# A graph layer with a fast Fourier convolution: PSUM tiles written whole before they are read, filter groups in tiles of their own, and one more adjacency turned by matrix multiply

## The chip, the cores and the metric
The kernel runs on one NeuronCore of a Trainium2 chip. The metric is the device time of one execution in microseconds; before the change the median of 14 runs is 1843.53 us (1836.01 to 1849.42). TensorE is PE in the profile, VectorE DVE, ScalarE ACT, GpSimd POOL, SyncE SP. SP computes nothing here: it only issues transfers. POOL issues transfers too, and ACT a few at the start.

## The reference
All data are float32. There are 64 graphs of 256 nodes with 256 features. Each is normalised and cut at zero, h = max(layernorm(x), 0), and then passes one layer:

```
xc  = transpose(h)                                  # features x nodes
c   = relu(bn1(conv1d(xc, conv1_w, 1 tap)))
c   = bn2(conv1d(c, conv2_w, 17 taps, pad 8))
x_conv = transpose(relu(c + xc))
s   = h @ w_se.T + b_se                             # 3 numbers per node
A   = exp(-|s_n - s_m|^2) * adj
x_nmp = A @ relu(h @ w_msg.T + b_msg)
gi  = concat(x_conv, x_nmp) @ w_ih.T + b_ih ; gh = h @ w_hh.T + b_hh
r, z = sigmoid(gi_r + gh_r), sigmoid(gi_z + gh_z)
n   = tanh(gi_n + r * gh_n)
out = x + (1 - z) * n + z * h
```

## The kernel before, in words
Graphs go in pairs (32 pairs) and batches of four pairs (8 batches). A batch's 17-tap convolution is done in a transformed domain: `split` and `forward` (VectorE) turn the output of the first convolution, `product` (TensorE) multiplies each of the 47 pieces of the spectrum with its filter matrix, and `branch_back`, `odd_back`, `q_back`, `p_back` and `join` (VectorE) turn back. `begin(m)` and `complete(m)` hold the products. Every product needs its own 256 KB matrix out of device memory, fetched by `load_kinds` (line 848) into one of nine slots named wb; a slot is loaded again when the product that used it is done.

**The filter matrices** are made at the start: `filters` (line 826) does two matmuls of the taps with constant points into a PSUM tile, ScalarE copies the tile to one of six buffers named fo, and a transfer, by turns from SP and POOL, writes it to device memory (filt). There are 57 such steps, taken from one list by `filter_steps` (line 1161) between other work.

**PSUM** is cut into four one-bank tiles (aux) and two two-bank tiles (acc), each kind handed out in a ring (lines 546 and 547). The dependencies are kept by tile: whoever writes one bank of an acc tile waits for the reader of its other bank.

**The adjacency.** `affinity(i)` (line 961) forms exp(-distance) on ScalarE and multiplies it by the adjacency on VectorE. The aggregation needs the product turned. For pairs below BY_DMA (line 589) the adjacency comes in as it is (`load_adj`, two transfers of 256 KB into the tile adj), and the product is turned on TensorE: eight 128x128 transposes and two ScalarE copies into the tile adjh (lines 975 to 982), where `aggregate` (line 986) reads it. For the other pairs the adjacency itself is turned on its way in: `turn_adj` (line 592) issues from SP a transposing transfer into the tile halves and four transfers to device memory (halves_d), `load_adj` fetches these into adjh with four transfers from POOL, and `join_adj` (line 610) makes the tile adj of them with two ScalarE copies.

**What sets the order of the work.** Every operation is first recorded, with its dependencies, and issued later by `emit`. The first `emit(True)` (line 1196), which covers the setup with the first four pairs' `transpose_h`, `conv1` and `split` and the first filter steps, issues in the order of the record. The other two calls (1209: the rest of the setup; 1361: all eight batches at once) go by a planner (line 375): it keeps a clock for each engine and issues whichever ready operation can start first, on each engine the one with the earliest due time. An operation on which nothing waits and which waits for nothing is ready from the beginning of its call, wherever it was recorded. `turn_h` (line 758) uses the tile halves too, so all transposing transfers follow one another in the order of the record.

Of the kernel before, what the change touches and what calls it, by code (L numbers as in the profile page):

```python
# [461 lines left out]
def kernel(  # L462
# [26 lines left out]
    DC = D // P  # L489
# [26 lines left out]
    def keep(name, *dims):  # L516
        return const.tile([P, *dims], FP, name=name)
# [28 lines left out]
    aux = Ring(psum.tile([P, W], FP, name=f"aux{k}") for k in range(4))  # L546
    acc = Ring(psum.tile([P, 2, W], FP, name=f"acc{k}") for k in range(2))
# [38 lines left out]

    BY_DMA = 3
    ADJD = {}  # L590

    def turn_adj(i):
        if i >= NP:
            return
        nc.sync.dma_start_transpose(out=halves, in_=adj[G * i:G * (i + 1)].rearrange("g n m -> (g n) m").bitcast(U16))
        ADJD[i] = halves_d()
        v = ADJD[i].rearrange("h q (k a) n -> k a (h q) n", a=4)
        for k in range(2 * MC):
            nc.sync.dma_start(out=v[k], in_=halves[:, k])

    def load_adj(i, eng=nc.gpsimd):
        if i >= NP:
            return
        if i < BY_DMA:
            load_rows(adj_rows, adj, i, eng)
            return
        for q in range(2 * MC):
            eng.dma_start(out=adjh[:, q], in_=ADJD[i][:, q])

    def join_adj(i):  # L610
        if not BY_DMA <= i < NP:
            return
# [174 lines left out]
    def conv1(i, both=None):  # L787
        if i >= NP:
            return
        p = acc() if both else None  # L790
        for o in range(DC):
            q = p[:, o] if both else aux()
            for k in range(DC):
                mm(q, w_c1[:, k, o * P:(o + 1) * P], HT[i][:, k, :], start=(k == 0), stop=(k == DC - 1))
            v = h1.rearrange("p (g o) s b -> p o g s b", o=DC)[:, o, :, :, 1:1 + NW]
            u = q.rearrange("p (g s b) -> p g s b", g=G, b=NW)
            if i == 0:
                nc.vector.tensor_scalar(v, u, s1[:, o:o + 1], h1_shift[:, o:o + 1], ALU.mult, ALU.add)
                nc.vector.tensor_scalar(v, v, 0.0, None, ALU.max)
            else:  # L800
                nc.scalar.activation(v, u, AF.Relu, bias=h1_shift[:, o:o + 1], scale=s1[:, o:o + 1])
# [159 lines left out]
    def affinity(i):  # L961
# [9 lines left out]
        for g in range(G):  # L971
            for c in range(MC):
                e = e_tile[:, g, c].rearrange("p (c h b) -> p c h b", c=MC, b=NW)
                nc.vector.tensor_mul(e, e, adj_rows[:, g * MC + c].rearrange("p (b h c) -> p c h b", c=MC, b=NW))
        if i < BY_DMA:
            at = adjh.bitcast(FP).rearrange("p a n -> p (a n)").rearrange("p (g c n) -> p g c n", g=G, c=MC)
            for g in range(G):
# [4 lines left out]
                nc.scalar.copy(at[:, g].rearrange("p c n -> p (c n)"), q)  # L982
        if i + 1 < BY_DMA:
            load_adj(i + 1)

    def aggregate(i):
# [3 lines left out]
        at = e_tile  # L990
        if i < BY_DMA:
            at = adjh.bitcast(FP).rearrange("p a n -> p (a n)").rearrange("p (g c n) -> p g c n", g=G, c=MC)
# [163 lines left out]
    FIRST = PARTS[1][1]  # L1156
    steps = deque((m, g) for g in range(FIRST) for m in range(len(PASSES)))
    steps.extend((m, g) for m in range(len(PASSES)) for g in range(FIRST, NG))
    banks = [0, None]

    def filter_steps(n):
        for _ in range(n):
            k = banks[0] % 4
            if k == 1:
                banks[1] = acc()
            banks[0] += 1
            p = aux() if k % 2 == 0 else banks[1][:, k // 2]
            filters(p, *steps.popleft(), nc.gpsimd if len(steps) % 2 else nc.sync)

    norm(0)  # L1170
# [5 lines left out]
    for j in range(PB):  # L1176
        if j > 0:
            transpose_h(j)
        if 0 < j < PB - 1:
            norm(j + 1)  # L1180
        if j == 2:
            nc.gpsimd.dma_start(out=w_msg[:, :, D:], in_=se_wT.rearrange("(k p) s -> p k s", p=P))
            for t, v in ((b_msg[:, :D], msg_b), (b_msg[:, D:], se_b)):
                nc.gpsimd.dma_start(out=t, in_=bass.AP(tensor=v.tensor, offset=v.offset, ap=[[0, P], [1, v.shape[0]]]))
            nc.sync.dma_start(out=w_msg[:, :, :D], in_=msg_wT.rearrange("(k p) o -> p k o", p=P))
            load_adj(0, nc.sync)
        conv1(j, True)
        if j == 2:
            *bn2, b_ih, b_hh = columns("bn2")
            s2, h2_shift = fold_bn(bn2, "bn2", 1.0 / L)  # L1190
            b_rz = keep("b_rz", 2 * DC)
            nc.vector.tensor_add(b_rz, b_ih[:, :2 * DC], b_hh[:, :2 * DC])
            nc.vector.tensor_scalar(b_rz, b_rz, 0.5, None, ALU.mult)
        split(j)
        filter_steps((4, 4, 2, 2)[j])
    nc.emit(True)
    load_x(PB)
    forward(0)
# [20 lines left out]
    for b in range(NB):  # L1219
        i = b * PB  # L1220
        nxt = i + PB
        if b > 0:
            finish(i - 1)
        begin(0)
        begin(1)
        complete(0)
        if b > 0:
            embed(i)
        complete(1)
        fft.branch_back(Yv, T, 0)  # L1230
        begin(2)
        if b > 0:
            affinity(i)
            load_adj(i + 1)
            give("tz0", "tz1")
        begin(3)
        complete(2)
        complete(3)
        if b == 0:
            norm(nxt)  # L1240
        fft.branch_back(Yv, T, 2)
        fft.odd_back(Yv, T)
        aggregate(i)
        begin(4)
        begin(5)
        if b > 0:
            join_adj(i + 1)
        else:
            nc.gpsimd.dma_start(out=w_hh, in_=hh_wT.rearrange("(k p) o -> p k o", p=P))
            nc.gpsimd.dma_start(out=w_ih, in_=ih_wT.rearrange("(k p) o -> p k o", p=P))  # L1250
            weight_sums()
        complete(4)
        message(i + 1)
        complete(5)
        fft.q_back(Yu, T)
        fft.odd_factors(Yv)
        begin(6)
        begin(7)
        embed(i + 1)
        if b == 0:  # L1260
            transpose_h(nxt)
            load_x(nxt + 1)
        else:
            join_h(nxt)
        complete(6)
        affinity(i + 1)
        if b > 0:
            load_adj(i + 2)
        complete(7)
        fft.p_back(Yu, T)  # L1270
        fft.q_factors(Yu)
        roles()
        sums(i, "h")
        sums(i, "xn")
        join(i)
        join(i + 1)
        if b == 0:
            turn_adj(3)
        stats(nxt + 1)
        aggregate(i + 1)  # L1280
        if b > 0:
            join_adj(i + 2)
        message(i + 2)
        conv1(nxt)
        split(nxt)
        turn_h(nxt + 1)
        embed(i + 2)
        sums(i, "xc")
        if b == 0:
            load_y(0)  # L1290
        else:
            load_adj(i + 3)
        sort_h(nxt + 1)
        turn_adj(nxt)
        join(i + 2)
        join(i + 3)

        def between():
            affinity(i + 2)
            join_h(nxt + 1)  # L1300
            stats(nxt + 2)
        gates(i, between)
        finish(i)
        for n in IN:
            sums(i + 1, n)
        conv1(nxt + 1)
        split(nxt + 1)
        if b + 1 < NB:
            forward(0)
        turn_h(nxt + 2)  # L1310
        aggregate(i + 2)
        if b == 0:
            load_adj(i + 3)
        sort_h(nxt + 2)
        turn_adj(nxt + 1)

        def between():
            join_h(nxt + 2)
            join_adj(i + 3)
            message(i + 3)  # L1320
            stats(nxt + 3)
        gates(i + 1, between)
        finish(i + 1)
        for n in IN:
            sums(i + 2, n)
        conv1(nxt + 2)
        split(nxt + 2)
        turn_h(nxt + 3)
        sort_h(nxt + 3)
        turn_adj(nxt + 2)  # L1330
        embed(i + 3)

        def between():
            affinity(i + 3)
            join_h(nxt + 3)
            conv1(nxt + 3)
            split(nxt + 3)
            if b + 1 < NB:
                forward(1)
            stats(nxt + 4)  # L1340
        gates(i + 2, between)
        finish(i + 2)
        turn_h(nxt + 4)
        aggregate(i + 3)
        for n in IN:
            sums(i + 3, n)
        sort_h(nxt + 4)
        turn_adj(nxt + 3)
        load_adj(nxt)
        if b + 1 < NB:  # L1350
            pending.extend(TURNS)

        def between():
            join_adj(nxt)
            message(nxt)
        gates(i + 3, between)
        give("axn", "axc", "ah")
        give("bh", "bxn", "bxc", "e")
        load_kinds()
# [47 lines left out]
```

## Time and profile before

| | |
|---|---|
| median of 14 runs | 1843.53 us (1836.01 to 1849.42) |
| profiled execution: device time, span of its trace | 1842.78 us, 1840.9 us |
| busy PE, DVE, ACT, POOL | 1733.7, 1505.1, 910.1, 240.6 us |
| PE busy in 0 to 120 us, 120 to 190 us, 190 to 300 us | 87.72, 60.21, 101.37 us |
| PE busy in seven windows of 210 us from 300 to 1770 us | 200.93 to 206.50 us |
| mean granted TensorE clock | 0.981 of full speed |

The span is the time from the first to the last instruction of the trace; 1.9 us of the device time lie around it. Nearly all operations are recorded through one helper, so all of them carry its line, L361, and are told apart by the tiles that they write and read: "acc<-V,wb" is a product of begin or complete, "acc<-hT,w_c" the first convolution, "aux<-taps,points" a filter step, "halves<-in_adj" the transposing transfer of turn_adj. A row of a timeline gives the start, the time taken, the operation with its count, and in brackets how long the engine stood idle before it and whom it waited for. "SPq" rows are SP's issuing of transfers, not the transfers themselves. A matmul in float32 shows as two records, so one product of 4 matmuls is 8 records.

### The profile page before, as it was taken

To read this page: it belongs to the slowest core of one execution; us is meant where nothing else is said; L and a number is where in the kernel's file an instruction comes from. 1 tells how busy PE (TensorE), PEld (TensorE's weight loads), DVE (VectorE), ACT (ScalarE), POOL (GpSimd) and SP (SyncE) were. 2 spreads that over 40 slices of the span, in tenths; PEclk is the share of its full clock that TensorE was granted. 3 is DMA by queue.
4 is the path that set the end of the run, shared out by engine and by line. 5 is a ranking of instruction groups with operands and counts; after the bars stand their busy time and mean duration, and the time that the engine had idled before them with its cause. 6 is when DMAs were issued, how large, how long until landed. Compare 5 with 4: busy or idle time off the path is not lost.

```text
span 1840.9 us, 26618 instructions
## 1 busy us (share of the span) xinstructions
PE 1733.7 (94%) x9190; PEld 1455.0 (79%) x9190; DVE 1505.1 (82%) x3462; ACT 910.1 (49%) x1763; POOL 240.6 (13%) x357
## 2 busy tenths in 40 slices
PE   4979989999999999999999999999999999999996
PEld 2659777787888878898878878888878878888885
DVE  3777987869978899789979799789979699789643
ACT  1544634455445564357454554447544564446331
POOL 2220031111011011011111100110211100110000
PEclk9999999999999999999999999999999999999998
DMA  7698245693347724494445824474444933264001
GB/s 182 196 213 252 63 110 116 162 246 79 81 108 191 212 48 107 87 279 110 110 110 169 237 64 88 107 228 145 108 112 119 266 100 81 58 189 138 24 23 35
DMA packets 250505, 246.25 MB, mean 134 GB/s; under 512 B 142936, under 2 KB 176500, under 8 KB 250371
## 3 DMA queue, kind: packets, MB, share of 16 engines
q1 hardware_dynamic: 216634, 183.83, 38.2%
q0 software_dynamic: 30784, 58.07, 12.6%
q10 hardware_dynamic: 2953, 2.66, 0.7%
q8 instruction: 72, 1.18, 0.3%
q14 instruction: 62, 0.51, 0.1%
HBM read 156.56 MB, written 44.30 MB: 109 GB/s over the span
## 4 chain that ended last, share of the span: by engine, by line
PE 50%; DVE 35%; DMA 7%; ACT 4%; issue 4%; SPq 1%; POOL 0%; ACTq 0%; DVEq 0%; POOLq 0%
PE acc L361 35%; PE aux L361 15%; DVE V L361 9%; DVE T L361 6%; DVE wb L361 3%; DVE U L361 3%; DVE tr L361 3%; DMA x<-in_x_dram 3%; DVE gn L361 3%; DMA wb<-filt 2%; DVE acc L361 2%; DVE msg L361 1%; DVE y L361 1%; DVE PT L361 1%; DVE Yv L361 1%
## 5 line engine op out<-in xcount | busy, mean ns | idle before, releaser
L361 PE MATMUL acc<-wb,w_ih 128*128 128x256 f32 x768 | 197.9, 380 | 0.0
L361 PEld LDWEIGHTS acc<-wb,w_ih 128*128 128x128 f32 x768 | 146.2, 190 | 20.0
L361 PE MATMUL aux<-wb,w_x 128*128 128x256 f32 x576 | 144.0, 382 | 4.7 <-DVE msg L361 3.6
L361 PE MATMUL acc<-wb,w_x 128*128 128x256 f32 x576 | 138.6, 383 | 5.9 <-DVE acc L361 5.9
L361 PE MATMUL acc<-V,wb 128*128 128x128 f32 x1024 | 130.9, 286 | 9.9 <-DMA wb<-filt 9.9
L361 DVE SCALAR_TENSOR_TENSOR V<-T,V 128x128 f32<-128x128 f32 (+2 forms) x448 | 138.7, 376 | 0.0
L361 PEld LDWEIGHTS acc<-V,wb 128*128 128x128 f32 x1024 | 128.0, 203 | 12.8 <-DMA wb<-filt 10.5
L361 PEld LDWEIGHTS acc<-wb,w_x 128*128 128x128 f32 x576 | 107.2, 190 | 35.7 <-DVE acc L361 15.6
L361 POOL DMA_DIRECT2D out_dram<-y x62 | 38.0, 616 | 732.3 <-DVE y L361 704.7
L361 PE MATMUL aux<-w_msg,hT 128*128 128x259 f32 x512 | 129.7, 383 | 0.6 <-ACT e L361 0.4
L361 PEld LDWEIGHTS aux<-wb,w_x 128*128 128x128 f32 x576 | 107.6, 190 | 28.3 <-DVE msg L361 6.7
L361 PE MATMUL acc<-hT,w_hh 128*128 128x256 f32 x384 | 110.1, 387 | 13.3 <-ACT acc L361 7.5
L361 PEld LDWEIGHTS acc<-U,wb 128*128 128x128 f32 x1024 | 119.2, 192 | 2.6 <-issue 1.3
L361 PE MATMUL acc<-U,wb 128*128 128x128 f32 x1024 | 120.8, 275 | 0.0
L361 POOL DMA_DIRECT2D adjh<-halves_d x116 | 69.1, 603 | 375.8 <-ACT adj L361 365.5
L361 PE MATMUL aux<-e,msg 128*128 128x256 f32 x464 | 114.5, 387 | 1.0 <-DVE e L361 1.0
L361 PE MATMUL acc<-wb,w_hh 128*128 128x256 f32 x384 | 110.4, 381 | 3.4 <-DVE acc L361 3.4
L361 PE MATMUL acc<-Yv,w_ih 128*128 128x256 f32 x384 | 110.1, 382 | 1.6 <-ACT Yv L361 1.6
L361 PE MATMUL aux<-hT,w_c 128*128 128x512 f32 x224 | 109.1, 595 | 2.1 <-ACT e L361 1.4
L361 DVE TENSOR_TENSOR acc<-acc,wb 128x512 f32<-128x512 f32 x64 | 44.3, 692 | 80.0 <-PE acc L361 79.8
L361 PE MATMUL acc<-xnm,w_ih 128*128 128x256 f32 x384 | 106.8, 380 | 0.0
L361 DVE BATCH_NORM_STATS2 st<-x 128x6 f32<-128x256 f32 x116 | 44.2, 417 | 76.6 <-DMA x<-in_x_dram 76.6
(175 smaller groups left out, 3877.6 us busy)
## 6 DMA issues: line engine op xcount, KB each, us to landing
wb<-filt SPq DMA_DIRECT2D x376, 256.0 KB
y<-in_x_dram POOLq DMA_DIRECT2D x64, 256.0 KB, 4.5
out_dram<-y POOLq DMA_DIRECT2D x62, 256.0 KB, 5.8
x<-in_x_dram SPq DMA_DIRECT2D x58, 256.0 KB
halves_d<-halves SPq DMA_DIRECT2D x116, 128.0 KB
adjh<-halves_d POOLq DMA_DIRECT2D x116, 128.0 KB, 3.3
hh<-halves SPq DMA_DIRECT2D x108, 128.0 KB
filt<-fo POOLq DMA_DIRECT2D x18, 252.0 KB, 4.9
```

Of the source, the lines that this page charges most:

```text
L361: self.tasks.append(Task(engine, lambda: method(*args, **kw), cost, size, self.first))
```

## The change
Three edits. The first convolution of a pair has two halves, each of two matmuls into one bank and one eviction; before, each half is evicted ahead of the matmuls of the next; now both banks are written and then both are read. A filter step no longer shares an acc tile with another step: two steps in three take an aux tile, the third an acc tile of its own, of which one bank is used; and two more of the 57 steps are put behind the second pair's first convolution, so two fewer are left for the second emit. The pair with number 3 is treated as pairs 0 to 2 are: its turn_adj and its own load_adj call are gone, join_adj does nothing for it, affinity(2) now ends by loading its adjacency, and affinity(3) turns its product on TensorE.

```diff
-    BY_DMA = 3
+    BY_DMA = 4
...
         p = acc() if both else None
-        for o in range(DC):
-            q = p[:, o] if both else aux()
+        qs = [p[:, o] if both else aux() for o in range(DC)]
+        for o, q in enumerate(qs):
             for k in range(DC):
                 mm(q, w_c1[:, k, o * P:(o + 1) * P], HT[i][:, k, :], start=(k == 0), stop=(k == DC - 1))
+        for o, q in enumerate(qs):
             v = h1.rearrange("p (g o) s b -> p o g s b", o=DC)[:, o, :, :, 1:1 + NW]
...
-    banks = [0, None]
+    banks = [0]
 
     def filter_steps(n):
         for _ in range(n):
-            k = banks[0] % 4
-            if k == 1:
-                banks[1] = acc()
             banks[0] += 1
-            p = aux() if k % 2 == 0 else banks[1][:, k // 2]
+            p = acc()[:, 0] if banks[0] % 3 == 0 else aux()
             filters(p, *steps.popleft(), nc.gpsimd if len(steps) % 2 else nc.sync)
...
-        filter_steps((4, 4, 2, 2)[j])
+        filter_steps((4, 6, 2, 2)[j])
...
         join(i + 1)
-        if b == 0:
-            turn_adj(3)
         stats(nxt + 1)
...
         aggregate(i + 2)
-        if b == 0:
-            load_adj(i + 3)
         sort_h(nxt + 2)
```

## The prediction
> **What bounds the kernel now.** I read the busy shares first: PE 94%, DVE 82%. From 300 us on PE stands idle 3.5 to 9.1 us in each 210 us (210 less the busy time of the windows); with so little to save there, a change that leaves PE's work as it is must be paid for at the start, where PE is busy 87.72 of 120, 60.21 of 70 and 101.37 of 110 us. So I went on to PE's waits and timelines up to 300 us. Three gaps touch the change. The first is in the setup, in PE's and DVE's timelines:
>
> ```profile
> 30.64 3.57 PE L361 MATMUL acc<-hT,w_c 128*128 128x512 f32 x4 [7.03 <-DVE h L361]
> ...
> 41.78 1.98 PE L361 MATMUL acc<-hT,w_c 128*128 128x512 f32 x4 [0.92 <-ACT h L361]
> ```
>
> ```profile
> 34.26 0.81 DVE L361 TENSOR_SCALAR h<-acc,bn_scale,bn_shift 128x512 f32<-128x512 f32 x1 [3.21 <-PE acc L361]
> ```
>
> The second half of a first convolution waits for the eviction of the first half: 7.03 us for pair 0, because VectorE still normalised pair 1, then 0.92, 0.87 and 0.87 us. DVE in turn waits 3.21 us for that second half. The second gap lies where the eight batches begin, in SP's and PE's timelines:
>
> ```profile
> 117.73 9.36 SPq L361 DMA_TRANSPOSE halves<-in_adj_dram  x1
> 127.20 14.17 SPq L361 DMA_DIRECT2D wb<-filt  x9
> ```
>
> ```profile
> 123.35 4.63 PE L361 MATMUL acc<-V,wb 128*128 128x128 f32 x40
> 127.81 0.60 PE L361 MATMUL aux<-adjh,msg 128*128 128x256 f32 x2
> 128.25 2.79 PE L361 MATMUL aux<-w_msg,hT 128*128 128x259 f32 x12
> 140.82 5.49 PE L361 MATMUL acc<-V,wb 128*128 128x128 f32 x24 [9.79 <-DMA wb<-filt]
> ```
>
> The transposing transfer of pair 3 heads SP's queue there: its issue alone holds the filter loads back for 9.36 us, and the first of them, issued at 127.20, lets PE go on only at 140.82. The windows (columns: length, PE, PEld, DVE, ACT, POOL busy, granted clock, DMA share, GB/s) show why so late:
>
> ```profile
> 124.00:126.00 2.00, 2.00 (x20) 2.00 (x19) 2.00 (x10) 0.17 (x1) 0.00 (x0) 1.00 0.96 346
> 132.00:134.00 2.00, 0.00 (x0) 0.00 (x0) 2.00 (x6) 0.00 (x0) 0.00 (x0) 1.00 1.16 70
> 138.00:140.00 2.00, 0.00 (x0) 0.00 (x0) 0.00 (x0) 0.00 (x0) 0.00 (x0) 0.50 0.70 101
> 142.00:144.00 2.00, 2.00 (x12) 2.00 (x11) 0.00 (x0) 0.00 (x0) 0.00 (x0) 0.50 1.06 389
> ```
>
> From about 127 to 140 us the DMA engines are full yet move 70 to 101 GB/s; before and after, 346 to 392. That is the transposing transfer. By its end the granted clock has fallen to 0.50, so the next products run slowly as well. The third gap is in ACT's and PE's timelines, in batch 0:
>
> ```profile
> 255.14 2.53 ACT L361 COPY adj<-adjh 128x1024 uint16<-128x1024 uint16 x2 [8.14 <-DMA adjh<-halves_d]
> ```
>
> ```profile
> 258.84 1.22 PE L361 MATMUL acc<-hT,w_hh 128*128 128x256 f32 x2 [5.77 <-ACT wb L361]
> ```
>
> ACT stands 8.14 us at the join of pair 3's adjacency, whose transfers POOL issued late (its pow on rstd took 7.29 us there against 1.03 elsewhere), and the gate evictions behind the join keep PE idle 5.77 us.
>
> **Part 1, first convolution and filter steps.** Nothing is added but order. For pair 0 both halves run from 21.63 us without a break; VectorE is free at 29.8, evicts both halves in turn (0.8 + 0.43 us each) by about 32.3 instead of 35.5: 3.2 us sooner. Three filter steps fill PE's old gap; the fourth takes the convolution's acc tile and waits for DVE until 31.9, and behind it on PE stands pair 1's transpose, which runs at about 33 instead of 37.55: still 4 us sooner. The two added filter steps cost PE 2 x 0.87 = 1.74 us ahead of pair 2 (0.87 by the spacing of the rows from 34.05 to 36.65). Pairs 1 to 3 save PE 0.9 us each, but ACT now evicts twice in a row at the end (2 x 0.79), so the pair itself ends only 0.9 + 0.0 to 0.4 sooner, less what the loads of x allow (pair 2's rows were in by 37.98, no sooner that I can see). Together the last split of the setup, at 62.41 us, starts 3.1 to 4.4 us sooner; I take 3.5. From there to the first product at 119.78 DVE's chain (47.1 us of work and 9.3 of waits) and PE's end together; the two steps fewer there shorten only PE's, so I count half of 1.74, 0.9. The false waits of PE on ACT's fo copies (4.8 us, twice) may go, but ACT itself waits there for the writes of fo, so I count nothing. **4.4 us**; at worst the two steps delay pair 2 and nothing else comes through, -1.7, at best all the idle time, 7.0 + 2.7 - 1.7 = 8.0.
>
> The Trainium skill, "PSUM — Partial Sum Buffer", Summary: rules for kernel authors, says that a PSUM read beside a running matmul only needs a different bank; by that, evicting one bank while the other is written should cost nothing, and writing both first would delay ACT by up to 0.8 us per pair. The rows of this kernel show the waits of 0.87 to 7.03 us instead, since the code keeps the order by tile. By the page alone this part would be a loss, estimated at 4 x 0.8 = 3.2 us.
>
> **Part 2, pair 3's transposing transfer.** It goes from the head of SP's queue, with four writes of halves_d between the filter loads (0.55 us of issue each). What is late next? The tenth product's slot is free after the first product, at 119.78 + 0.9 = 120.7; its load can start there. Ahead of the loads stand w_hh and w_ih (2.3 MB, issued by POOL at 117.2) and the first rows of y (0.5 MB): 2.8 MB at 380 GB/s are 7.4 us, so even behind all of it the first load lands before 131.0, where PE has finished its nine ready products, the aggregation and the message. PE needs 256 KB per 0.89 us, 288 GB/s, which the 380 to 392 GB/s cover. No other transposing transfer can move up: turn_adj(4) is tied to the tile halves behind turn_h(5), which needs rows of x. PE thus goes on at 131.0 and not 140.82: 9.8 us. At the full clock 24 records take 24 x 0.116 = 2.8 and not 5.5 us (0.116 from 40 records in 4.63): 2.7 us. Sum 12.5. From 147 us DVE's turning back, which waits for these products, is as full as PE (9.7 of 10 us), so DVE must move too: its work on the sums of w_hh and w_ih ends at 134.5, its wait for ACT begins there and ends at 147.0, so it has 12.5 us to give, less about 1 if w_hh lands later among the filter loads. **11.5 us**, bounds 10 and 12.5.
>
> The Trainium skill, "DMA: Bandwidth & Descriptors", Latency and other measured facts, gives a DMA transpose 261 GB/s. At that price the 512 KB of one pair would take an estimated 2 us, the loads would hardly be held up beyond the issue, and this part would bring some 3 us. The windows above, 70 to 101 GB/s for about 12 us, speak for the larger figure.
>
> **Part 3, pair 3's adjacency in batch 0.** Gone: four POOL fetches into adjh and two ACT copies (2 x 1.33 us), with ACT's 8.14 us wait. Added: two POOL loads of 256 KB into adj behind affinity(2) (its last multiply ends at 208.8; such loads landed in 4.3 to 7.6 us; pair 3's multiply is at 289, so they are hidden by 70 us); eight PE transposes, 8 x 0.13 = 1.0 us (1.03 for the eight of 37.55); two ACT copies of 0.59. The gate evictions then come when PE writes them, as at 216 to 219 us, where PE waited 0.48: 5.77 - 0.48 = 5.3 us, bounds 0 (the next gate step is late anyway) and 5.8. The transposes cost PE **1.0**. A wait is added: adjh now holds pair 3's turned product until aggregate(3) ends at 314.4, so pair 4's fetch, at 256.77 before, comes 58 us later; its multiply is at 357.1, so 30 to 40 us still cover the fetch (3 to 12 us) and the join (2.5).
>
> **Sum**: 4.4 + 11.5 + 5.3 - 1.0 = 20.2 us, against the profiled execution's own 1842.78 (span 1840.9 and 1.9 around it; the median is 0.75 higher): **1822.6 us**. Bounds: -1.7 + 10 + 0 - 1.0 = 7.3, so 1835.5; 8.0 + 12.5 + 5.8 - 1.0 = 25.3, so 1817.5. All later work hangs on earlier work and on nothing that stands at a fixed time, so the gain should last to the end.
>
> **Rivals.**
> A, the setup gives nothing: writing 57 filter groups sets its pace. For it: ACT waits for the writes of fo at 69, 71 and 103 us. Against: the DMA engines are only 0.43 to 0.49 busy from 40 to 70. It takes 4.4 away: 1827.0.
> B, the join's stall moves to pair 4: its fetch now stands late on POOL, whose queue waits for DVE's y up to 23 us at a time, and ACT would again stand at the join with gate evictions behind it. The price is the stall of before, 5.8: 1828.4.
> C, the other side: the planner lays out all eight batches in one call, so the whole later order may differ. Place: the seven windows from 300 us, idle 9.1, 7.2, 3.5, 5.8, 4.2, 6.2, 5.8 us, 41.7 in all. If each were as the worst, 7 x 9.1 = 63.7, the price is 22. With the full gain that ends at 1844.6, no change; with the least, 7.3, at 1857: slower. It decides when the mean idle time per window passes 9.3 us with the full gain, 7.5 with the least. Against it: the products of batches 3 to 8 begin 209 and 214 us apart by turns, a pattern that the order falls back into.
> D, the same mechanism the other way: each window as the best, 7 x 3.5 = 24.5, gains 17: 1805.
>
> **Chances.** Forecast 0.53, A 0.12, B 0.15, D 0.07, C 0.13, of which 0.05 ends within 0.2% and 0.08 slower. Faster by over 0.2% (3.7 us, about what a measurement can tell from no change) is 0.53 + 0.12 + 0.15 + 0.07 = 0.87, within it 0.05, slower 0.08. The range takes in the forecast, A, B and the bounds of the costs, with a few us of changed order below: 1811 to 1836, 0.80.
>
> **What would show it.** Right: PE's 7.03 us gap before the second half of pair 0 is gone and the first product starts near 115; no transposing transfer on SP between setup and first filter loads; the gap before the tenth product under 2 us with the clock at 1.00; no 8 us wait of ACT at a join near 240; the start of the second batch's products (351.04 before) near 331. Wrong: filter loads that still land at 13 us, a gap at aggregate(3) or at pair 4's join, or windows after 300 us with more idle time than 9 us.

## The result
The changed kernel takes 1811.54 us (median of 10 runs) against 1841.77 (48 runs): ratio 0.9837, 95% interval 0.9822 to 0.9853, some 30 us less. The forecast was 20.2 us less, with a range of 1811 to 1836. The time lies inside that range by 0.5 us, and that is luck, since a third of the gain came from where the sum has no term. The direction and the three gaps were right, the size was not: the places that I had counted came to about what was forecast, and 10 us (by the medians) to 14 us (by the two traces) more came from batches where I had counted nothing.

To see where, I compare the two profiled executions (spans 1840.9 and 1807.3 us) by one landmark, the start of each batch's first product ("acc<-Sv,wb" in PE's timeline):

| us | before | after | difference | forecast |
|---|---|---|---|---|
| start to first product | 119.8 | 114.0 | -5.8 | -4.4 |
| batch 0 | 231.2 | 217.2 | -14.0 | -15.8 |
| batch 1 | 220.8 | 213.5 | -7.3 | 0 |
| batches 2 to 7, to the end | 1269.1 | 1262.6 | -6.5 | 0 |

PE's timeline of the changed kernel in the setup (start, time taken, operation, and in brackets the idle time before it):

```profile
22.82 3.93 PE L361 MATMUL acc<-hT,w_c 128*128 128x512 f32 x8
26.59 1.03 PE L361 MATMUL acc<-taps,points 119*77 119x256 f32 x4
...
33.07 1.55 PE L361 MATMUL acc<-taps,points 119*77 119x256 f32 x4 [3.73 <-DVE h L361]
```

Both halves of pair 0's first convolution run in one piece of 8 records, filter steps follow at once, and the fourth of them waits 3.73 us for DVE: that is what is left of the gap of 7.03 us. (The three dots stand for one row of two more filter steps.) SP's timeline where the batches begin:

```profile
91.62 20.01 SPq L361 DMA_DIRECT2D filt<-fo  x9
115.08 42.13 SPq L361 DMA_DIRECT2D wb<-filt  x38
```

No transposing transfer stands between the last filter writes and the filter loads. PE's timeline of the same kernel there, and its windows (columns as in the prediction):

```profile
117.57 4.63 PE L361 MATMUL acc<-V,wb 128*128 128x128 f32 x40
123.46 1.16 PE L361 MATMUL acc<-V,wb 128*128 128x128 f32 x8 [1.26 <-DMA wb<-filt]
126.56 3.78 PE L361 MATMUL acc<-V,wb 128*128 128x128 f32 x16 [1.94 <-DMA wb<-filt]
```

```profile
118.00:120.00 2.00, 2.00 (x20) 2.00 (x19) 2.00 (x11) 0.40 (x1) 0.00 (x0) 1.00 1.01 405
...
122.00:124.00 2.00, 0.74 (x6) 0.55 (x6) 2.00 (x11) 0.47 (x1) 0.40 (x1) 1.00 1.01 221
...
130.00:132.00 2.00, 2.00 (x11) 2.00 (x11) 0.95 (x2) 1.07 (x2) 0.00 (x0) 0.50 0.89 280
```

Of the wait of 9.79 us, 3.2 are left, in two pieces, and the granted clock still falls to 0.50 for some 6 us. The last of the three gaps is gone: between 225 and 262 us PE waits for nobody, and pair 4's join, which I feared, waits 1.13 us in ACT's timeline:

```profile
302.25 2.68 ACT L361 COPY adj<-adjh 128x1024 uint16<-128x1024 uint16 x2 [1.13 <-DMA adjh<-halves_d]
```

Batch 1, by windows, of the kernel before and of the changed one:

```profile
351.00:571.80 220.80, 213.97 (x1112) 179.62 (x1113) 183.63 (x424) 110.80 (x211) 26.48 (x40) 0.97 0.53 130
```

```profile
331.20:544.70 213.50, 209.33 (x1113) 176.43 (x1113) 184.77 (x422) 111.17 (x214) 23.93 (x38) 0.99 0.53 135
```

The same 1112 or 1113 matmul records keep PE busy 213.97 us in one and 209.33 in the other: 4.6 of the 7.3 us are not waits but a lower granted clock (0.97 against 0.99, the third number from the end of each row).

### The profile page after: what moved, and what is told of

Its sections match the earlier page's. It is cut to its first block, busy times and chain, and to the rows that moved or that the text cites. A ratio compares the mean times of both kernels' runs of the same rounds, so it can differ in the third digit from the quotient of the medians.

```text
span 1807.3 us, 26629 instructions
## 1 busy us (share of the span) xinstructions
PE 1724.6 (95%) x9198; PEld 1451.0 (80%) x9198; DVE 1505.7 (83%) x3462; ACT 908.1 (50%) x1763; POOL 242.8 (13%) x355
## 4 chain that ended last, share of the span: by engine, by line
PE 43%; DVE 36%; ACT 3%; issue 3%; DMA 3%; SPq 0%; ACTq 0%; DVEq 0%
PE acc L361 30%; PE aux L361 13%; DVE V L361 9%; DVE T L361 5%; DVE wb L361 4%; DVE tr L361 3%; DVE U L361 3%; DVE gn L361 3%; DVE acc L361 3%; DVE PT L361 1%; DVE msg L361 1%; DMA wb<-filt 1%; DVE y L361 1%; ACT zT L361 1%; DMA x<-in_x_dram 1%
## 5 line engine op out<-in xcount | busy, mean ns | idle before, releaser
L361 PE MATMUL acc<-V,wb 128*128 128x128 f32 x1024 | 126.7, 281 | 3.7 <-DMA wb<-filt 3.5
L361 PEld LDWEIGHTS acc<-V,wb 128*128 128x128 f32 x1024 | 123.1, 197 | 6.2 <-DMA wb<-filt 4.6
L361 PE MATMUL aux<-e,msg 128*128 128x256 f32 x448 | 109.9, 387 | 0.6 <-DVE e L361 0.6
L361 PEld LDWEIGHTS aux<-w_msg,hT 128*128 128x128 f32 x512 | 94.5, 190 | 15.6 <-ACT fo L361 1.2
```

What stands on the lines that cost most here:

```text
L361: self.tasks.append(Task(engine, lambda: method(*args, **kw), cost, size, self.first))
```

## The experiments
**Theory 1**: each part gives what its own place shows, and the later batches differ because the planner lays all eight out in one call and any edit ahead of it or in it gives another order. **Rival 2**: the extra belongs to the adjacency path of pairs 3 and 4. **Rival 3**: it belongs to the setup's edits. All of these kernels, the base included, were timed in several rounds; ratios are to the kernel before.

### One edit at a time
The first convolution alone (both banks written, then both read):

```diff
-        for o in range(DC):
-            q = p[:, o] if both else aux()
+        qs = [p[:, o] if both else aux() for o in range(DC)]
+        for o, q in enumerate(qs):
...
+        for o, q in enumerate(qs):
```

> The kernel before with the first convolution alone changed (both banks written, then both read). Theory 1 (each part works where it stands, and the later batches change only as the planner happens to lay them out): the first product starts 3 to 4 us before 119.78 us, PE's 7.03 us gap of pair 0 is gone, and the whole time falls by 3 to 4 us, give or take the later order (up to 10). Rival (the setup is paced by writing the filter groups): the first product stays within 1 us of 119.78.

The filter steps alone:

```diff
-            p = aux() if k % 2 == 0 else banks[1][:, k // 2]
+            p = acc()[:, 0] if banks[0] % 3 == 0 else aux()
...
-        filter_steps((4, 4, 2, 2)[j])
+        filter_steps((4, 6, 2, 2)[j])
```

> The kernel before with the filter steps alone changed (own tiles, two more steps behind pair 1). Theory 1: the first product starts about 1 to 2 us sooner, since both halves of pair 0's convolution still wait for DVE and the two added steps find no gap of their own before pair 2. Rival (the false waits on shared tiles set the pace): 4 us or more.

Pair 3's adjacency alone:

```diff
-    BY_DMA = 3
+    BY_DMA = 4
...
-        if b == 0:
-            turn_adj(3)
...
-        if b == 0:
-            load_adj(i + 3)
```

> The kernel before with pair 3's adjacency alone changed. Theory 1: the first product stays at 119.8 within 1 us; batch 0 takes about 14 us less (217 where it took 231), and the whole time falls by 14, give or take the later order. Rival 2 (the rest of the gain, some 10 us behind batch 0, belongs to the adjacency path of pairs 3 and 4): the whole falls by 24 or more.

The first two edits together, pair 3 as before:

> The kernel before with the convolution and the filter steps changed, pair 3 as before. Theory 1: the first product starts 5.8 us sooner, as in the changed kernel; the 13 us landing of the filter loads is still there; the whole time falls by 6, give or take the later order. Rival 3 (the later gain comes with the setup's edits): it falls by 14 or more.

| kernel | ratio (interval) | first product | batch 0 | batches 1 to 7 |
|---|---|---|---|---|
| before | 1 | 119.8 | 231.2 | 1489.9 |
| convolution alone | 0.9920 (0.9888 to 0.9951) | 121.7 | 228.5 | 1479.1 |
| filter steps alone | 0.9943 (0.9922 to 0.9964) | 118.5 | 232.3 | 1485.2 |
| pair 3 alone | 0.9909 (0.9885 to 0.9933) | 122.5 | 220.9 | 1480.8 |
| both setup edits | 0.9911 (0.9882 to 0.9940) | 112.5 | 228.2 | 1482.7 |

The landmarks are of one profiled execution each. Alone, neither setup edit moves the first product by more than the executions differ (the setup is the same code before and with pair 3 alone, 119.8 and 122.5), so the 3 to 4 us expected of the convolution are not there; together they move it by 7.3, a single figure that this scatter puts in doubt. The last split of the setup is steadier: it starts at 62.41 us before, 60.83 with the convolution, 64.41 with the filter steps, 57.73 with both. The reason stands in PE's timeline with the convolution alone, where the next filter step still shares its acc tile with the step before it:

```profile
44.06 2.07 PE L361 MATMUL acc<-taps,points 119*126 119x256 f32 x4 [4.46 <-ACT fo L361]
```

ScalarE's copy out of that tile comes late, at 43.41 us, because ScalarE had itself stood 4.38 us for a write of fo; with both edits PE no longer waits there. With the filter steps alone, pair 0's second half still waits:

```profile
30.33 3.78 PE L361 MATMUL acc<-hT,w_c 128*128 128x512 f32 x4 [7.24 <-DVE h L361]
```

So the two belong together. But the whole times fall by 14.7 and 10.5 us with one edit each, 16.8 with pair 3 alone: 42 in sum for a change worth 30, and in each of them batches 1 to 7, which none of the setup edits touches, are 5 to 11 us shorter than before. Rivals 2 and 3 each name one part as the owner of the later gain, and every edit brings some of it. Rival 2 asked for 24 us and got 16.8. Rival 3 asked for 14 us of both setup edits and got 16.4, so its figure was met here; with the order held fixed, below, it was not.

The setup's edits also reach into Part 2. With both of them and pair 3's transfer still at the head of the queue, PE's wait for the filter loads is 4.67 us and not 9.79 (5.95 with the convolution alone, 8.87 with the filter steps alone).

### The transposing transfer, by itself
Pair 3's adjacency by the transposing transfer as before, recorded behind that of pair 5's rows:

```diff
         join(i + 1)
-        if b == 0:
-            turn_adj(3)
...
         sort_h(nxt + 1)
+        if b == 0:
+            turn_adj(3)
         turn_adj(nxt)
```

> The kernel before, in which pair 3's adjacency still comes by the transposing transfer, but recorded behind that of pair 5's rows, so that it leaves the head of SP's queue. All later orders stay nearly the same. Theory 1: PE's 9.8 us gap and the half clock behind it go, batch 0 takes 10 to 12 us less, the join's wait of ACT stays, the whole time falls by 10 to 12. Rival (w_hh, w_ih and y take its place in front of the filter loads): less than 4.

Ratio 0.9925 (0.9900 to 0.9950), 14 us less (9 to 18 by the interval), for the transposing transfer and its four writes of halves_d moved; batch 0 takes 222.0 us, 9.2 less. At its new place the same transfer holds SP for 1.91 us and not 9.36. PE's timeline, a window, and ACT's wait at the join:

```profile
127.68 2.05 PE L361 MATMUL acc<-V,wb 128*128 128x128 f32 x16 [1.88 <-DMA wb<-filt]
```

```profile
128.00:130.00 2.00, 2.00 (x20) 2.00 (x19) 0.17 (x1) 0.18 (x1) 0.00 (x0) 1.00 1.06 388
```

```profile
244.03 2.66 ACT L361 COPY adj<-adjh 128x1024 uint16<-128x1024 uint16 x2 [7.25 <-DMA adjh<-halves_d]
```

The wait for filter loads is 1.88 us and the clock stays at 1.00, while the join's wait is as it was. DVE's turning back, its first "T<-Yv", starts 15.5 us after the first product and not 27.2: the full 11.8 (before rounding). By the first gate matmul 6.1 of them are left (64.9 and not 70.9 us after the first product), since DVE, busy 42.7 of 43.7 us in that stretch before, now has 47.3 of 49.4 to do there; 3.1 come back up to the end of the batch.

The reverse, the changed kernel with the transposing transfer put back, its result read by nobody:

```diff
         join(i + 1)
+        if b == 0:
+            nc.sync.dma_start_transpose(out=halves, in_=adj[6:8].rearrange("g n m -> (g n) m").bitcast(U16))
         stats(nxt + 1)
```

> The changed kernel with the transposing transfer of pair 3's adjacency put back at the head of SP's queue, its result read by nobody; the four writes of halves_d are not there. Theory 1: the filter loads land some 13 us late again and the time is 9 to 12 us above the changed kernel, about 1822. Rival (at the 261 GB/s that the Trainium skill's page DMA: Bandwidth & Descriptors gives such a transfer, an estimate): 2 to 3 us above it.

and with a plain transfer of the same size there:

```diff
         join(i + 1)
+        if b == 0:
+            nc.sync.dma_start(out=halves.rearrange("p k w -> p (k w)"),
+                              in_=adj[6:8].rearrange("g (p r) m -> (g p) (r m)", r=4).bitcast(U16))
         stats(nxt + 1)
```

> As the kernel with the spare transposing transfer, but a plain transfer of the same 512 KB into the same tile at the same place. If it is the transposing that costs: 1 to 2 us above the changed kernel, its share at the rate of plain transfers (0.5 MB at 380 GB/s is 1.4 us). If it is the place at the head of the queue: as much as the transposing one, 9 us or more.

They give 0.9879 (0.9853 to 0.9905) and 0.9869 (0.9844 to 0.9893): 7.7 and 5.9 us above the changed kernel, with some 5 us of uncertainty each. Batch 0 takes 223.0 and 220.6 us, against 217.2. SP's and PE's timelines with the transposing transfer, then the same two with the plain one:

```profile
111.30 10.39 SPq L361 DMA_TRANSPOSE halves<-in_adj_dram  x1
121.78 18.45 SPq L361 DMA_DIRECT2D wb<-filt  x18
```

```profile
128.72 5.49 PE L361 MATMUL acc<-V,wb 128*128 128x128 f32 x24 [4.12 <-DMA wb<-filt]
```

```profile
112.30 0.50 SPq L361 DMA_DIRECT2D halves<-in_adj_dram  x1
115.90 23.61 SPq L361 DMA_DIRECT2D wb<-filt  x19
```

```profile
124.54 1.16 PE L361 MATMUL acc<-V,wb 128*128 128x128 f32 x8 [0.20 <-DMA wb<-filt]
128.07 1.16 PE L361 MATMUL acc<-V,wb 128*128 128x128 f32 x8 [2.37 <-DMA wb<-filt]
130.36 2.08 PE L361 MATMUL acc<-V,wb 128*128 128x128 f32 x8 [1.14 <-DMA wb<-filt]
```

The issue of the transposing transfer holds SP 10.39 us, that of the plain one 0.50. Still the wait that follows is 4.12 us and not 9.79: here the transfer begins 3.8 us ahead of the first product, 2.1 before, and no write of halves_d follows. With the plain transfer PE waits nearly as long, 3.71 us in three pieces, and the changed kernel with neither waits 3.2. So neither the totals nor PE's waits tell the two apart, and these kernels do not show that transposing itself is what costs; that both carry another order of batch 0 than the changed kernel blurs them. What is shown is the worth of moving the transfer together with its four writes (9.2 us of batch 0, above); how that divides between the transposing, the writes and the place in the queue stays open.

### The order held fixed
To take the planner out, it is made to forget its clocks ahead of the call that lays out the batches:

```diff
+    def fresh(self):
+        for t in self.tasks[:self.planned]:
+            t.done = 0.0
+        self.dma = 3.0
+        self.lanes = [deque([0.0] * self.LANES) for _ in range(2)]
+        self.free = dict.fromkeys(self.LAG, 0.0)
...
     finish(NP - 1)
+    nc.fresh()
     nc.emit()
```

> The kernel before, but the planner forgets its clocks ahead of the call that lays out the eight batches, so their order no longer depends on the setup. It serves as the base of the next two. Theory 1 (an order is worth up to 20 us by itself): its time may lie anywhere from 1825 to 1865.

> The same with the first convolution and the filter steps changed; the order of all eight batches is then identical, instruction for instruction, to that of its base. Theory 1 (the two edits are worth only what the first product shows, the rest of their 16 us was the planner's other order): 4 to 7 us below its base, and the length from the first product to the end the same within 3 us. Rival 3 (the edits themselves shorten the batches): 14 us or more below its base.

> The changed kernel, whole, with the planner's clocks forgotten in the same way. Theory 1: batch 0 is 10 to 15 us shorter than in the kernel with the setup's edits alone, the later batches differ by the order, up to 10 us either way. Rival 2: 24 us or more below it.

Medians are 1837.61, 1829.81 and 1819.76 us; ratios 0.9975 (0.9953 to 0.9997), 0.9933 (0.9909 to 0.9958) and 0.9874 (0.9848 to 0.9900). The first two have one order: from the first product on, the operations of ACT and DVE are the same, one by one. Between them the setup's edits are worth 7.8 us, give or take 6 (from the two intervals), and not 16.4 or the 14 of Rival 3.

But these 7.8 us do not lie where they were expected. In the traces (the first is of an execution 4.5 us above its kernel's median) the first product starts only 2.6 us sooner, where 4 to 7 were expected, and the rest, expected the same within 3 us, is 9.8 us shorter: 6.4 in batch 0 and 5.7 in batch 1 (224.2 and 218.5 us, at a granted clock of 0.95 and 0.98), while the later batches are 2.3 longer. So what Rival 3 says, that the setup's edits themselves shorten batches, holds in part, at less than its size. PE's wait for the filter loads, without and with the setup's edits:

```profile
138.01 4.53 PE L361 MATMUL acc<-V,wb 128*128 128x128 f32 x24 [7.77 <-DMA wb<-filt]
```

```profile
130.25 2.94 PE L361 MATMUL acc<-V,wb 128*128 128x128 f32 x24 [2.60 <-DMA wb<-filt]
```

The transposing transfer stands ahead of these loads in both, so in one and the same order the setup's edits take away 5.2 us of what Part 2 had counted for removing it. Why the loads land sooner was not settled.

The third kernel is 10 us below the second, give or take 7. Pair 3's path is part of the batches, so here the order changes with the edit, and the 10 us are both together; batch 0 is 6.4 us shorter, where 10 to 15 were expected. In sum the three kernels span 17.9 us, against 30 with the clocks kept. The third has no wait for filter loads in batch 0 at all: its planner put the aggregation and the message between the ninth product and the later ones, as I had supposed. In turn PE stands 4.12 us just ahead of its first product and begins at half clock (6.29 us for the first 32 records, 3.73 in the changed kernel).

### The order alone
One number of the planner, on the kernel before and on the changed one:

```diff
-    LAG = {"tensor": 0.25, "vector": 0.14, "scalar": 0.16, "gpsimd": 0.2, "sync": 0.0}
+    LAG = {"tensor": 0.25, "vector": 0.16, "scalar": 0.16, "gpsimd": 0.2, "sync": 0.0}
```

> The kernel before with one number of the planner changed (VectorE's lag from 0.14 to 0.16 us) and nothing else: the same work in another order. Theory 1 (the order alone moves the later batches): the time moves by 3 to 10 us in either direction, mostly behind 350 us, with other waits for filter loads and other stretches at a low granted clock. Rival (the order is worth nothing): within 3 us.

> The changed kernel with the same one number of the planner changed (VectorE's lag 0.16 us). Theory 1 (an order moves the batches by up to 20 us, and the change's own parts are worth about 18): slower than the changed kernel by anything from 0 to 25 us, with first product and batch 0 as in the changed kernel within 5 us, and the difference behind batch 0. Rival (the changed kernel's order is settled, the batches fall back into one pattern): within 3 us of the changed kernel.

They take 1864.49 us, ratio 1.0113 (1.0091 to 1.0135), and 1845.65 us, ratio 1.0014 (0.9993 to 1.0035). The same work in another order costs 22 us on the kernel before and 34 on the changed one, which is then no faster than the kernel before without it; both are more than was expected (3 to 10, and 0 to 25). Under this planner the change is worth 18.8 us by the medians. In the traces it lies in other places than the forecast had it: 11.3 us up to the first product (125.8 and 114.5 us), 7.4 in batch 0, and batches 1 to 7 are 4.0 longer. So that it comes near 20.2 proves nothing. PE's waits for filter loads over the whole span (total, times, longest, in us), first of the changed kernel, then of the changed kernel under the other number:

```profile
PE acc L361 <- DMA wb<-filt: 3.7, 5, 1.9
```

```profile
PE acc L361 <- DMA wb<-filt: 35.7, 10, 8.3
```

That is 32 of the 40.8 us by which these two traces differ: an order in which products meet their loads too soon. Its batches 1 to 7 take 1516.3 us, against 1476.1. Of the kernel before the same count goes from 17.8 to 24.7 us only, so its 22 us have other waits in them, which were not followed up.

## Why the prediction was right in sign and short in size
- **Part 1, 4.4 us: right in the mean.** The last split starts at 57.7 to 59.7 us in six kernels with both edits and at 62.4 to 63.8 in four with the setup as before (the two of the other number left out), 4.0 sooner in the mean (forecast 3.1 to 4.4). The first product starts at 113.8 and 118.2 us in their means, 4.4 sooner, but with a scatter as wide as that (112.6 to 115.1 and 115.0 to 122.5). With the order held the total is 7.8, with an interval that takes in 4.4, though in that pair of traces only 2.6 of it came at the first product. Rival A, that the setup gives nothing, is out. I had not seen that the two edits need one another, nor that they shorten the wait that Part 2 counts whole (9.79 to 4.67 us, and 7.77 to 2.60 in one order): the parts do not simply add.
- **Part 2, 11.5 us: the mechanism is right, the size was put too high.** Moving the transfer alone shortens batch 0 by 9.2. What I got wrong is that nothing would wait. At 122 us the DMA engines were full at 221 GB/s, where I had reckoned with 380; and of the message, which before kept PE busy up to 131.0, six records now run ahead of the first product and the others later, so PE comes to the tenth product at 122.2. It waits 3.2 us, and the half clock returns. And 6 of the 12 us at the start of the turning back are lost again before the first gate, as DVE is the fuller engine there. The Trainium skill, "DMA: Bandwidth & Descriptors", Latency and other measured facts, has 261 GB/s for a DMA transpose with a non-contiguous middle dimension. The estimate of 3 us worked out from it is short of the 9.2 us here, and the windows of 70 to 101 GB/s lie below it; but since the spare transposing transfer cost PE hardly more than the plain one, no run here measures the transfer's own rate.
- **Part 3, 5.3 - 1.0 us: the stall went, the size stays open.** All eight kernels with pair 3 by transfer show PE waits of 4.2 to 7.1 us behind that join, the six others have neither that join nor that wait. But three of the six (pair 3 alone and the two with a spare transfer) wait 2.65 to 4.14 us for ACT at an earlier gate step, at 210 to 219 us. From the first gate to the end of batch 0 the changed kernel takes 150.9 us, pair 3 alone 156.0 and the late transfer, which has the stall, 157.2; between 1 and 6 us is all that these say, the late transfer compared with each of the other two. Rival B, that the stall moves to pair 4, came to 1.13 us of ACT's time.
- **The step that failed is the one that has no term in the sum**: it took the windows after 300 us to stay as before ("the gain should last to the end", and no more), with Rival D (order gains 17) at 0.07 and Rival C (order loses 22) at 0.13 beside it. Batches 1 to 7 became 13.8 us shorter in the profiled executions. I took the pattern of 209 and 214 us by turns for a settled order. It is settled, but in two phases: before, batches 2, 4 and 6 are the long ones; after, batches 1, 3 and 5. The same pattern thus has one long batch less from batch 2 on, and that is about the 6.5 us in the table's last row. The other traces bear this out. From batch 2 on, the operations of ACT and DVE have only two orders in the twelve kernels under the first number: the kernel before, the late transfer and the first two with clocks forgotten share one, the changed kernel and the other seven share the other. In the first, batch 2 to the end takes 1269.1 to 1273.3 us, 1271.4 in the mean; in the second 1261.8 to 1271.6, 1265.8 in the mean. So the order is worth some 6 us there, about half of what came uncounted. (That the 30 us exceed both the 17.9 with clocks forgotten and the 18.8 under the other number by some 12 is no measure of the order: in neither pair is it held.)
- **Batch 1's 7.3 us** are less clear. The kernel with the late transfer has the order of the kernel before again from some 60 us into that batch, and yet takes 212.5 and not 220.8 us, with a granted clock of 1.00 and not 0.97; and the two kernels with one order and clocks forgotten take 224.2 and 218.5. So it isn't the order alone. Before, PE waited 4.04 us for a filter load at 351 and ran slowly after, which points to when the loads land; why they landed later was not settled, and this other half of the uncounted gain stays open.
- The **rivals of the experiments**: one edit that owns the later gain (2 and 3) was not found, since every edit brought some of it. Rival 3 holds in part: in one order the setup's edits made batches 0 and 1 shorter, and Theory 1 is not all that there is.

## What to carry to other kernels
Where a planner orders a long stretch in one go, an edit ahead of it is also a new order, and here an order alone moved the time by 22 and 34 us, as much as the whole change: time an edit ahead of the stretch with the order held, by making the planner forget what came before, and try the edit under a second setting of the planner before crediting it. An edit inside the stretch cannot be held in this way. Gains that meet at one wait do not add: here the setup's edits took away half or more of the wait that the third edit was meant to remove. An operation that waits for nothing is issued first by such a planner, wherever it was recorded; a transfer of that kind that later loads queue behind belongs behind something that holds it back, which alone brought 14 us. And two false waits on shared tiles in one stretch may have to be removed together before either shows.

## What the runs showed of the hardware
- The length of a short wait does not tell whether the half clock follows. The wait of 1.88 us in the kernel with the late transfer left the granted clock at 1.00. In the same trace a single one of 2.01 us was followed by 0.50, as these rows of PE's timeline and of the windows show:

```profile
178.16 1.86 PE L361 MATMUL aux<-w_msg,hT 128*128 128x259 f32 x4 [2.01 <-ACT xnm L361]
```

```profile
178.00:180.00 2.00, 1.84 (x5) 1.48 (x6) 1.85 (x5) 1.67 (x4) 0.00 (x0) 0.61 0.85 179
180.00:182.00 2.00, 2.00 (x5) 1.17 (x4) 2.00 (x5) 0.00 (x0) 0.00 (x0) 0.54 1.02 214
```

With both setup edits a wait of 1.60 us at 195 us was followed by 0.50 and another of 1.60 at 301 was not; one of 2.60 (setup's edits, clocks forgotten) and one of 2.90 us (spare transposing transfer) were not either. Of the 30 waits of 3.7 us and more between 100 and 1780 us, in all fourteen traces, every one was. The Trainium skill, "TensorE: Matmul & The Clock Gate", What's actually happening, puts the half clock after at least one idle window of about 3.4 us; the 30 agree with that, the waits of 1.60 and 2.01 us do not.
- The DMA engines can be fully busy at very different rates without any transposing transfer: 405 GB/s at 118 to 120 us and 221 at 122 to 124 in the changed kernel, both with a share of 1.01. Which transfer is the slow one was not separated.
- Issuing a transposing transfer of one and the same size held SP for anything from 1.7 to 9.4 us in the kernel before (29 of in_adj, median 2.2); the 9.36 us ahead of the filter loads is the longest, and not a fixed price.
- The same setup code reached the first product at 119.8, 122.5, 115.0 and 115.4 us in four executions (before, pair 3 alone, late transfer, clocks forgotten). A setup gain of 4 us can't be read from one pair of traces.
